# Attention's score rows spread over partitions through lines in DRAM, and a planner with other settings

## The chip, the cores and the metric

The kernel runs on one core of one Trainium2 chip. The metric is the device time of one execution in microseconds (us), the median of several runs. The core has five engines, each with a queue of its own that runs in order: PE (TensorE, matmuls; its weight loads are shown as PEld), DVE (VectorE), ACT (ScalarE), POOL (GpSimd) and SP (SyncE), which here only issues transfers (DMA). Engines meet through semaphores: an instruction that waits holds up everything behind it in its engine's queue.

## The reference

There are 128 graphs of 128 nodes with 256 features each, in float32, and an adjacency of 0 and 1 per graph. Four layers follow each other, each as `x = x + layer(relu(layernorm(x)))`.

```python
# layer 0: three GRU steps over the graph
m = einsum('bnd,de->bne', h, weight[i]); aggr = einsum('bst,bsd->btd', A, m)
h = gru_cell(aggr, h, w_ih, w_hh, b_ih, b_hh)
# layer 1: sum over neighbours by relation (adj holds the relation), times weight, plus bias
h = einsum('rbnm,bmd->rbnd', masks, x); y = einsum('rbnd,rdo->bno', h, weight) + bias
# layers 2 and 3: graph attention
Wh = einsum('bnd,od->bno', h, W)
e = leaky_relu((Wh @ a1)[:, :, None] + (Wh @ a2)[:, None, :], 0.2)
out = einsum('bij,bjo->bio', softmax(where(adj, e, -inf or -9e15)), Wh)
```

The score `e[i, j]` is the sum of one number of node i and one number of node j. With node i on the partition, the first is a number per partition, which an activation adds as its bias. The second is needed as a row of 128 numbers, the same on all partitions. The change is about how that row comes about.

## The kernel before

**Tiling.** Four graphs form a group (G = 4), so there are 32 groups (NG). A group's features are one tile of 128 x 4 x 256 in the pool `xs` (five buffers); its adjacency and the transposed adjacency come from `adjs` (seven). Intermediate 128 x 512 tiles come from `big` (27), statistics and small columns from `small` (ten), and PE writes into eight PSUM banks. `load` issues a group's four transfers on SP, and a store at the end of the group (L1096) writes the result.

**One group.** Layer 0 runs three GRU steps, whose matmuls are made of seven products in place of eight (`seventh`, L820); their bank is refilled several times, with a copy (`evict`, L330, on ACT or on DVE as the planner finds) or an add (L843, L898, L912) between. Layer 1 is `neighbours` (L624, L639). Layers 2 and 3 are `attention` with two masks. In `attention`, `norm` makes the normalised features (statistics on DVE from L532, one power on POOL at L558, the scaling on ACT at L574). Then `terms` (L993, DVE) takes two dot products per graph, which give the node's two score numbers as columns EI and EJ of a small tile. In `attend` the row is made on PE: a transpose of the column EJ, broadcast along the free dimension, against the identity (L1018). It lands in a bank, the same row on every partition. An activation adds EI (L1023, ACT); then follow the slope (L1027, DVE), the mask with a minimum (L1030), the exponential with its sum (L1036, ACT), the transpose of the weights (L1054, PE), two products (L1065, L1078) and the weighted add to the features (L1088, DVE).

**What sets the order.** Nothing is issued as it is written. `Plan.op` records each operation with an estimated duration; `Plan.order` then plays the program through and picks the next operation that could start first on its engine, by rank where several could. The rank is the group's number times PERIOD, less the length of the way to the group's end. At most AHEAD groups are open at once. SPARE keeps back buffers of some pools from groups that are not the oldest. LAG, HOP and OWN are the estimated times until the result of one engine is seen by another, or by itself. The order that comes out is written into the engines' queues and stays fixed. The last SPLIT groups are worked in two pieces of two graphs rather than whole.

**The branch.** A scan of the whole adjacency (32 transfers and reductions, L508 and L510) finds out whether it holds values above 1. The verdict (L513 to L519) goes to a branch: with 0 and 1 alone, layer 1 is `neighbours`; else the general `relations`. Work up to layer 0 is shared by both sides and may stand ahead of the branch.

Of the kernel before, what the change touches and what calls it, by code (L numbers as in the profile page):

```python
# [37 lines left out]
OWN = {"PE": 0, "ACT": 125, "DVE": 125, "POOL": 80, "SP": 0, "ACTQ": 0}  # L38
PERIOD = 28000
AHEAD = 4  # L40
SPLIT = 3
SPARE = (1, 0, 0, 3)
# [4 lines left out]
def seen(o, h):  # L47
    return LAG[o.eng] + HOP[h.eng] if h.engs != (o.eng,) else OWN[o.eng]


def act(n, ptrs=0):
    return 50 + 95 * ptrs + 0.833 * n


def dve(n):
    return 68 + n / 0.96
# [21 lines left out]
class Op:  # L78
    __slots__ = ("engs", "eng", "times", "ns", "fn", "deps", "heirs", "bufs", "group", "key", "port", "rank", "wait", "ready", "end")
# [12 lines left out]
class Plan:  # L92
# [6 lines left out]
    def op(self, eng, ns, fn, r=(), w=(), after=(), port=None):  # L99
# [4 lines left out]
        o.port = eng == "POOL" if port is None else port  # L104
        if self.shared:
            o.key = self.keys
            self.keys += 1
# [21 lines left out]
    def order(self, pools, cut=None, prefix=()):  # L129
# [37 lines left out]
        def place(o, eng, end):  # L167
# [85 lines left out]
def kernel(  # L253
# [40 lines left out]
    pools = [banks, xs, adjs, big, wide, half, small, mis]  # L294
# [3 lines left out]
    def build(general):  # L298
# [38 lines left out]
        def chunk(name):  # L337
            return Buf(big, name)
# [167 lines left out]
        for f in range(F):  # L506
# [7 lines left out]
            top.t[:, 0:1], most.t, AX.X, ALU.max), r=[most], w=[top])  # L514
        op("PE", 109, lambda: nc.tensor.transpose(pm.t[0:1, 0:P], top.t[:, 0:1], ident.t),
           r=[top, ident], w=[pm])
        op("DVE", 200, lambda: nc.vector.tensor_reduce(
            top.t[0:1, 1:2], pm.t[0:1, 0:P], AX.X, ALU.max), r=[pm], w=[top])
        verdict = op("DVE", 80, lambda: nc.vector.tensor_scalar(  # L519
            found, top.t[0:1, 1:2], 1.0, None, ALU.is_gt), r=[top])  # L520
# [5 lines left out]
        whole = (range(G),)  # L526

        def norm(xt, nm, pieces=whole):
# [39 lines left out]
            hs = []  # L568
            for g2 in range(G // 2):
                h = chunk(f"h{nm}{g2}")  # L570

                def scale(g2=g2, h=h):
                    for g in (2 * g2, 2 * g2 + 1):
                        nc.scalar.activation(  # L574
                            h.t[:, (g % 2) * D : (g % 2 + 1) * D], xt.t[:, g, :], AF.Relu,
                            bias=s.t[:, MR + g : MR + g + 1], scale=s.t[:, RS + g : RS + g + 1],
                        )

                op("ACT", 2 * act(D, 2) + 85, scale,
                   r=[(xt, {2 * g2, 2 * g2 + 1}), (s, {(n, g) for n in ("rs", "mr") for g in (2 * g2, 2 * g2 + 1)})], w=[h])  # L580
                hs.append(h)
# [16 lines left out]
        def bias(xt):  # L598
            for g2 in range(G // 2):
                op("POOL", 1370, lambda g2=g2: nc.gpsimd.tensor_tensor(  # L600
                    xt.t[:, 2 * g2 : 2 * g2 + 2, :], xt.t[:, 2 * g2 : 2 * g2 + 2, :],
                    b1s.t.unsqueeze(1).to_broadcast([P, 2, D]), ALU.add),
                   r=[b1s], w=[(xt, {2 * g2, 2 * g2 + 1})])
# [7 lines left out]
        def neighbours(gi, xt, ai, aiT, m0, m3, late, pieces):  # L611
# [4 lines left out]
            hs, _ = norm(xt, f"1_{gi}", pieces)  # L616
            bias(xt)
            for g2 in range(G // 2):
                pr = bank(f"pr{gi}{g2}")

                def gather(g2=g2, pr=pr):
                    for g in range(2):
                        for k in range(KC):
                            nc.tensor.matmul(  # L624
                                pr.t[:, (2 * k + g) * P : (2 * k + g + 1) * P],
                                hs[g2].t[:, g * D + k * P : g * D + (k + 1) * P],
                                mT.t[:, (2 * g2 + g) * P : (2 * g2 + g + 1) * P],
                                start=True, stop=True,
                            )

                op("PE", 892, gather, r=[hs[g2], mT], w=[pr])
                hr = chunk(f"hr{gi}{g2}")
                evict(T, lambda hr=hr: hr.t, lambda pr=pr: pr.t, r=[pr], w=[hr])
                py = bank(f"py{gi}{g2}")

                def mix(hr=hr, py=py):
                    for g in range(2):
                        for k in range(KC):
                            nc.tensor.matmul(  # L639
                                py.t[:, g * D : (g + 1) * D],  # L640
                                hr.t[:, (2 * k + g) * P : (2 * k + g + 1) * P],
                                w1s.t[:, k, :],
                                start=(k == 0), stop=(k == KC - 1),
                            )

                op("PE", 2 * KC * 2 * D * PE_COL, mix, r=[hr, w1s], w=[py])
                op("DVE", dve(T), lambda g2=g2, py=py: nc.vector.tensor_tensor(
                    xt.t[:, 2 * g2 : 2 * g2 + 2, :], xt.t[:, 2 * g2 : 2 * g2 + 2, :],
                    py.t.rearrange("p (g d) -> p g d", g=2), ALU.add),
                   r=[py], w=[(xt, {2 * g2, 2 * g2 + 1})])  # L650

        def relations(gi, xt, ai, aiT, m0, m3, late, pieces):
# [55 lines left out]
        def group(gi):  # L708
# [272 lines left out]
            pieces = (range(2), range(2, G)) if gi >= NG - SPLIT else whole  # L981
            (relations if general else neighbours)(gi, xt, ai, aiT, m0, m3, late, pieces)
            unrelated(m2, m0, FAR, late)

            def attention(i, mask):
                hs, s = norm(xt, f"{2 + i}_{gi}", pieces)

                EI, EJ = 48, 52
                for g in range(G):
# [9 lines left out]
                    op("DVE", 690, terms, r=[hs[g // 2], ub[i]], w=[junk, (s, {("ei", g)})], port=True)  # L999
# [3 lines left out]
            def attend(i, mask, hs, s, gs, EI, EJ):  # L1003
# [9 lines left out]
                pe, e = bank(f"pe{nm}"), chunk(f"e{nm}")  # L1013
# [7 lines left out]
                op("PE", 110 * len(gs), rows, r=[ident, (s, {("ei", g) for g in gs})], w=[pe])  # L1021
                for g in gs:
                    op("ACT", 250, lambda g=g: nc.scalar.activation(  # L1023
                        at(e, g), at(pe, g), AF.Identity, bias=s.t[:, EI + g : EI + g + 1]),
                       r=[pe, (s, {("ei", g)})], w=[(e, {g})])
# [33 lines left out]
                for g2 in range(gs.start // 2, gs.stop // 2):  # L1059
                    pc, c, po = bank(f"pc{nm}{g2}"), chunk(f"cT{nm}{g2}"), bank(f"po{nm}{g2}")  # L1060

                    def weigh(g2=g2, pc=pc):
                        for g in range(2):
                            for k in range(KC):
                                nc.tensor.matmul(  # L1065
                                    pc.t[:, (2 * k + g) * P : (2 * k + g + 1) * P],
                                    hs[g2].t[:, g * D + k * P : g * D + (k + 1) * P],
                                    at(eT, 2 * g2 + g),
                                    start=True, stop=True,
                                )  # L1070

                    op("PE", 892, weigh, r=[hs[g2], eT], w=[pc])
                    evict(T, lambda c=c: c.t, lambda pc=pc: pc.t, r=[pc], w=[c])

                    def transform(c=c, po=po):
                        for g in range(2):
                            for k in range(KC):
                                nc.tensor.matmul(  # L1078
                                    po.t[:, g * D : (g + 1) * D],
                                    c.t[:, (2 * k + g) * P : (2 * k + g + 1) * P],  # L1080
                                    wa[i].t[:, k, :],
                                    start=(k == 0), stop=(k == KC - 1),
                                )

                    op("PE", 2 * KC * 2 * D * PE_COL, transform, r=[c, wa[i]], w=[po])
                    for g in range(2):
                        gg = 2 * g2 + g
                        op("DVE", 395, lambda g=g, gg=gg, po=po: nc.vector.scalar_tensor_tensor(  # L1088
                            xt.t[:, gg, :], po.t[:, g * D : (g + 1) * D], s.t[:, RI + gg : RI + gg + 1],
                            xt.t[:, gg, :], ALU.mult, ALU.add),  # L1090
                           r=[po, (s, {("rinv", gg)})], w=[(xt, {gg})])
# [69 lines left out]
```

## Time and profile before

| what | us |
|---|---|
| median of three runs | 2647.51 (2646.8 to 2647.52) |
| the profiled execution | 2648.33 |
| its span, first to last instruction | 2646.5 |
| ACT busy | 1566.5 (59%) |
| POOL busy | 466.0 (18%) |
| 128 transfers of 256 KB for features and adjacency, issue to landing | 4.0 to 4.5 each |
| 29 stores of 512 KB | 3.3 each |

The profile comes from one execution. A group of instructions is shown by its line in the kernel, its engine, and its tiles. "Busy" counts the time in which an engine has an instruction under way; on PE instructions overlap, so the mean duration of one is longer than the time from one start to the next. The chain of waits is followed back from the last instruction, at each step to what released it, or to the instruction before it on its engine; what stands in it is what the end depended on. SP's queue in this kernel mostly stands still: it waited 2057.4 us in total before stores (L1096) for the last add of a group on DVE (L1088).

### The profile page before, as it was taken

How to read it: one execution, taken by the hardware profiler on the slowest of the kernel's cores; microseconds unless marked ns; L12 is line 12 of the kernel's file. 1: busy time of each engine (PE TensorE's matmuls, PEld its weight loads, DVE VectorE, ACT ScalarE, POOL GpSimd, SP SyncE). 2: the span in 40 equal slices, each digit the busy share in tenths (PEclk: the TensorE clock that was granted, in tenths of full speed). 3: DMA queues.
4: the chain of work that ended last, by engine and by line, in shares of the span. 5: the costliest groups of instructions: out<-in, count | busy, mean ns of one | idle time of the engine just before them, and what ended most of it. 6: DMA issues, size and time to landing. Idle time of an engine off the chain costs nothing.

```text
span 2646.5 us, 40354 instructions
## 1 busy us (share of the span) xinstructions
PE 2606.2 (98%) x14041; PEld 2321.0 (88%) x14041; DVE 2204.8 (83%) x6376; ACT 1566.5 (59%) x3792; POOL 466.0 (18%) x400
## 2 busy tenths in 40 slices
PE   8999999999999999999999999999999999999995
PEld 7888888888888888988898988888888889888884
DVE  8868898888888888888888888888888888888885
ACT  5446666656566565565565656565656655665553
POOL 1112122111121111121111111111111111211121
PEclk9999999999999999999999999999999999999997
DMA  6100000000000000000000000000000000000000
GB/s 208 42 1 1 29 21 25 25 25 25 10 16 25 25 25 25 1 25 25 25 25 25 1 25 25 25 25 21 5 25 25 25 25 2 24 25 25 9 9 18
DMA packets 77494, 65.22 MB, mean 25 GB/s; under 512 B 3936, under 2 KB 73184, under 8 KB 77280
## 3 DMA queue, kind: packets, MB, share of 16 engines
q1 hardware_dynamic: 76192, 61.50, 7.8%
q8 instruction: 112, 1.84, 0.3%
q10 hardware_dynamic: 1088, 1.05, 0.1%
q14 instruction: 102, 0.84, 0.1%
HBM read 45.75 MB, written 16.78 MB: 24 GB/s over the span
## 4 chain that ended last, share of the span: by engine, by line
PE 94%; DVE 4%; ACT 1%; issue 0%; DMA 0%; POOL 0%; ACTq 0%; DVEq 0%
PE bank L820 64%; PE bank L1078 8%; PE bank L1065 4%; PE bank L762 4%; PE bank L639 4%; PE bank L954 3%; PE bank L733 2%; PE bank L624 2%; PE bank L1054 1%; PE bank L1018 1%; DVE junk L993 0%; PE bank L445 0%; DVE small L532 0%; DVE big L922 0%; DVE big L942 0%
## 5 line engine op out<-in xcount | busy, mean ns | idle before, releaser
L330 ACT COPY big<-bank 128x512 f32<-128x512 f32 (+1 forms) x978 | 455.5, 481 | 496.7 <-PE bank L820 426.3
L820 PE MATMUL bank<-big,rz_h 128*128 128x256 f32 x1536 | 462.8, 383 | 0.3
L820 PE MATMUL bank<-big,rz_a 128*128 128x256 f32 x1536 | 456.8, 379 | 0.0
L929 POOL TENSOR_TENSOR big<-wide,big 128x512 f32<-128x512 f32 x192 | 245.6, 1298 | 1108.7 <-ACT big L927 951.6
L820 PE MATMUL bank<-wide,rz_h 128*128 128x256 f32 x1152 | 342.9, 379 | 0.3 <-DVE wide L330 0.3
L820 PE MATMUL bank<-wide,rz_a 128*128 128x256 f32 x1152 | 342.6, 379 | 0.0
L820 PEld LDWEIGHTS bank<-big,rz_a 128*128 128x128 f32 x1536 | 291.8, 190 | 39.8
L820 PEld LDWEIGHTS bank<-big,rz_h 128*128 128x128 f32 x1536 | 279.7, 190 | 47.3 <-ACT big L330 15.0
L558 POOL TENSOR_TENSOR small<-small,nhalf 128x4 f32<-128x4 f32 (+1 forms) x137 | 138.8, 1014 | 970.4 <-DVE small L556 951.6
L574 ACT ACTIVATE big<-xs,small 128x256 f32<-128x256 f32 x512 | 269.8, 592 | 48.4 <-DVE small L562 48.0
L837 ACT ACTIVATE big<-big,b_rz 128x256 f32<-128x256 f32 x576 | 258.2, 499 | 44.3 <-DVE big L843 42.1
L330 DVE COPY big<-bank 128x512 f32<-128x512 f32 (+1 forms) x276 | 159.9, 581 | 143.8 <-PE bank L820 89.3
L927 ACT ACTIVATE big<-big,bih_s 128x512 f32<-128x512 f32 x192 | 128.7, 715 | 205.4 <-DVE big L912 109.1
L820 PEld LDWEIGHTS bank<-wide,rz_a 128*128 128x128 f32 x1152 | 218.9, 190 | 29.7
L820 PEld LDWEIGHTS bank<-wide,rz_h 128*128 128x128 f32 x1152 | 216.3, 190 | 28.5 <-DVE wide L330 0.5
L1078 PE MATMUL bank<-wa,big 128*128 128x256 f32 x1024 | 235.5, 383 | 2.6 <-ACT big L330 2.6
L843 DVE TENSOR_TENSOR big<-bank,big 128x512 f32<-128x512 f32 x288 | 196.2, 686 | 47.3 <-PE bank L820 46.8
L820 PE MATMUL bank<-big,n_h 128*128 128x256 f32 x768 | 228.2, 380 | 0.8 <-DVE big L330 0.7
L1078 PEld LDWEIGHTS bank<-wa,big 128*128 128x128 f32 x1024 | 195.0, 191 | 30.6 <-ACT big L330 4.2
L820 PE MATMUL bank<-big,n_a 128*128 128x256 f32 x768 | 217.9, 379 | 0.0
L912 DVE TENSOR_TENSOR big<-bank,big 128x256 f32<-128x256 f32 x384 | 160.6, 419 | 61.6 <-PE bank L820 57.9
L993 DVE CUSTOM_DVE_ANT_0 junk<-big,ub 128x256 f32<-128x256 f32 x512 | 192.6, 421 | 1.6 <-ACT big L574 1.5
(91 smaller groups left out, 4723.0 us busy)
## 6 DMA issues: line engine op xcount, KB each, us to landing
xs<-in_x_dram SPq DMA_DIRECT2D x64, 256.0 KB, 4.0
out_dram<-xs SPq DMA_DIRECT2D x29, 512.0 KB, 3.3
adjs<-in_adj_dram SPq DMA_DIRECT2D x32, 256.0 KB, 4.3
adjs<-in_adjT_dram SPq DMA_DIRECT2D x32, 256.0 KB, 4.5
big<-in_adj_dram SPq DMA_DIRECT2D x32, 256.0 KB, 3.0
out_dram<-xs SPq DMA_DIRECT2D x6, 256.0 KB, 2.2
big<-in_wihT_dram ACTq DMA_DIRECT2D x3, 256.0 KB, 6.4
big<-in_whhT_dram SPq DMA_DIRECT2D x3, 256.0 KB, 5.8
```

The source lines that it names most:

```text
L330: (nc.scalar.copy if eng == "ACT" else nc.vector.tensor_copy)(dst(), src())
L558: op("POOL", 1130, lambda: nc.gpsimd.tensor_tensor(columns(RS), columns(RS), nhalf.t[:, gs.start : gs.stop], ALU.pow), r=[nhalf], w=[own(" ...
L574: nc.scalar.activation(h.t[:, (g % 2) * D : (g % 2 + 1) * D], xt.t[:, g, :], AF.Relu, bias=s.t[:, MR + g : MR + g + 1], scale=s.t[:, RS + ...
L639: nc.tensor.matmul(py.t[:, g * D : (g + 1) * D], hr.t[:, (2 * k + g) * P : (2 * k + g + 1) * P], w1s.t[:, k, :], start=(k == 0), stop=(k = ...
L820: nc.tensor.matmul(ps.t[:, m * W : (m + 1) * W], a.t[(slice(None), *row, j, slice(m * P, (m + 1) * P))], b[j](), start=(start and m == x = ...
L837: op("ACT", act(W, 1) + 40, lambda m=m, c=c: nc.scalar.activation(t[c].t[:, g2 * W : (g2 + 1) * W], src.t[:, m * W : (m + 1) * W], AF.Tanh ...
L843: op("DVE", dve(T), lambda: nc.vector.tensor_tensor(c.t, ps.t, c.t, ALU.add), r=[ps], w=[c])
L912: op("DVE", dve(W), lambda: nc.vector.tensor_tensor(dst(), ps.t[:, :W], dst(), ALU.add), r=[ps], w=[((ws if more else vs)[c], {g2})])
L927: op("ACT", act(T, 1) + 85, lambda nn=nn, c=c: nc.scalar.activation(nn.t, vs[c].t, AF.Tanh, bias=bi.t[:, 4 + c : 5 + c]), r=[vs[c], bi], w ...
L929: op("POOL", 1230, lambda qq=qq, nn=nn, c=c: nc.gpsimd.tensor_tensor(qq.t, hT.t[:, c, :], nn.t, ALU.subtract), r=[(hT, {(c, 0), (c, 1)}), ...
L993: nc.vector.tensor_tensor_reduce(out=junk.t[:, v * D : (v + 1) * D], in0=part, in1=ub[i].t[:, v, :], op0=ALU.mult, op1=ALU.add, scale=1.0, ...
L1078: nc.tensor.matmul(po.t[:, g * D : (g + 1) * D], c.t[:, (2 * k + g) * P : (2 * k + g + 1) * P], wa[i].t[:, k, :], start=(k == 0), stop=(k ...
```

## The change

The row no longer comes from PE for a group that is worked whole. SP writes the four columns EJ of the group (128 partitions x 4 floats, 16 bytes each) to a small tile in DRAM, `line`, so that the four numbers of a node stand next to each other. A second transfer reads this line of 2 KB once for each of the 128 partitions into a tile of `big`. The row of one graph is then every fourth float of it, and the activation that adds EI reads it with that step. There are four lines. Groups in pieces keep the transpose.

The planner's estimates get `late`, a time added to LAG for one operation: 5000 ns for the line, 2500 for the spread. An operation on SP that depends on another on SP now counts with 2500 in place of 0. PERIOD goes from 28000 to 26000, AHEAD from 4 to 5, SPLIT from 3 to 2, and SPARE no longer keeps a bank back. The four operations of the verdict get a rank that is 60000 earlier. Scaling, bias and the products are rewritten so that they could also run on single graphs; with SINGLE = 0 none does, and they run on pairs as before. The two products of layer 1 and of attention now share the function `product`.

```diff
-OWN = {"PE": 0, "ACT": 125, "DVE": 125, "POOL": 80, "SP": 0, "ACTQ": 0}
-PERIOD = 28000
-AHEAD = 4
-SPLIT = 3
-SPARE = (1, 0, 0, 3)
+OWN = {"PE": 0, "ACT": 125, "DVE": 125, "POOL": 80, "SP": 2500, "ACTQ": 2500}
+PERIOD = 26000
+AHEAD = 5
+SINGLE = 0
+SPLIT = 2
+LINE, SPREAD = 5000, 2500
+RUSH = 60000
+SPARE = (0, 0, 0, 3)
...
 def seen(o, h):
-    return LAG[o.eng] + HOP[h.eng] if h.engs != (o.eng,) else OWN[o.eng]
+    return o.late + (LAG[o.eng] + HOP[h.eng] if h.engs != (o.eng,) else OWN[o.eng])
...
-            o.rank = o.group * PERIOD - o.rank
+            o.rank = o.group * PERIOD - o.rank - o.rush
...
-                    last = max(u.end + LAG[u.eng] + 60 for u, _, _ in b.uses)
+                    last = max(u.end + u.late + LAG[u.eng] + 60 for u, _, _ in b.uses)
...
+    dram = ctx.enter_context(tc.tile_pool(name="dram", bufs=1, space=bass.MemoryType.DRAM))
+    lines = [dram.tile([P, G], F32, name=f"line_{j}") for j in range(4)]
+    pools = [banks, xs, adjs, big, wide, half, small, mis, lines]
...
         verdict = op("DVE", 80, lambda: nc.vector.tensor_scalar(
-            found, top.t[0:1, 1:2], 1.0, None, ALU.is_gt), r=[top])
+            found, top.t[0:1, 1:2], 1.0, None, ALU.is_gt), r=[top], rush=RUSH)
...
+        def product(gs, nm, hs, r, weight, w):
+
+            N = len(gs) * D
+            pc, c, po = bank(f"pc{nm}"), chunk(f"c{nm}"), bank(f"po{nm}")
+            op("PE", 446 * len(gs), lambda: sums(gs, pc, hs, weight),
+               r=[(hs[gs.start // 2], set(gs)), r], w=[pc])
+            evict(N, lambda: c.t[:, :N], lambda: pc.t[:, :N], r=[pc], w=[c])
+            op("PE", len(gs) * KC * 2 * D * PE_COL, lambda: mix(gs, po, c, w), r=[c, w], w=[po])
+            return po
...
-            pieces = (range(2), range(2, G)) if gi >= NG - SPLIT else whole
-            (relations if general else neighbours)(gi, xt, ai, aiT, m0, m3, late, pieces)
+            pieces = singly if gi >= NG - SINGLE else pairs if gi >= NG - SPLIT else whole
+            duos = singly if gi >= NG - SINGLE else pairs
+            (relations if general else neighbours)(gi, xt, ai, aiT, m0, m3, late, pieces, duos)
...
-                pe, e = bank(f"pe{nm}"), chunk(f"e{nm}")
+                e = chunk(f"e{nm}")
...
-                op("PE", 110 * len(gs), rows, r=[ident, (s, {("ei", g) for g in gs})], w=[pe])
+                terms = (s, {("ei", g) for g in gs})
+                if len(gs) == G:
+
+                    line, pe = Buf(lines, f"line{nm}"), chunk(f"pe{nm}")
+                    op("SP", 400, lambda: nc.sync.dma_start(out=line.t, in_=columns(EJ)),
+                       r=[terms], w=[line], late=LINE)
+                    op("SP", 1280, lambda: nc.sync.dma_start(
+                        out=pe.t, in_=line.t.rearrange("p g -> (p g)").partition_broadcast(P)),
+                       r=[line], w=[pe], late=SPREAD)
+
+                    def row(g):
+                        return pe.t[:, g : g + (P - 1) * G + 1 : G]
+                else:
+                    pe = bank(f"pe{nm}")
+                    op("PE", 110 * len(gs), rows, r=[ident, terms], w=[pe])
+
+                    def row(g):
+                        return at(pe, g)
                 for g in gs:
                     op("ACT", 250, lambda g=g: nc.scalar.activation(
-                        at(e, g), at(pe, g), AF.Identity, bias=s.t[:, EI + g : EI + g + 1]),
-                       r=[pe, (s, {("ei", g)})], w=[(e, {g})])
+                        at(e, g), row(g), AF.Identity, bias=s.t[:, EI + g : EI + g + 1]),
+                       r=[(pe, {g}), (s, {("ei", g)})], w=[(e, {g})])
```

More of the change, by code (lines that the diff above doesn't have):

```diff
@@ L78 @@
 class Op:
-    __slots__ = ("engs", "eng", "times", "ns", "fn", "deps", "heirs", "bufs", "group", "key", "port", "rank", "wait", "ready", "end")
+    __slots__ = ("engs", "eng", "times", "ns", "fn", "deps", "heirs", "bufs", "group", "key", "port", "rush", "late", "rank", "wait", "ready", "end")
     def __init__(self, engs, times, fn, group):
@@ L97, in __init__, with op @@
         self.keys = 0
-    def op(self, eng, ns, fn, r=(), w=(), after=(), port=None):
+    def op(self, eng, ns, fn, r=(), w=(), after=(), port=None, rush=0, late=0):
         o = Op(*((eng, ns) if isinstance(eng, tuple) else ((eng,), (ns,))), fn, self.group)
         o.port = eng == "POOL" if port is None else port
+        o.rush, o.late = rush, late
         if self.shared:
@@ L293 @@
     mis = pool(4, [P, G + 1, P], F32R, "mis")
-    pools = [banks, xs, adjs, big, wide, half, small, mis]
+    dram = ctx.enter_context(tc.tile_pool(name="dram", bufs=1, space=bass.MemoryType.DRAM))
+    lines = [dram.tile([P, G], F32, name=f"line_{j}") for j in range(4)]
+    pools = [banks, xs, adjs, big, wide, half, small, mis, lines]
     found = const.tile([1, 1], I32, name="found")
@@ L513, in build, with norm @@
         op("DVE", 120, lambda: nc.vector.tensor_reduce(
-            top.t[:, 0:1], most.t, AX.X, ALU.max), r=[most], w=[top])
+            top.t[:, 0:1], most.t, AX.X, ALU.max), r=[most], w=[top], rush=RUSH)
         op("PE", 109, lambda: nc.tensor.transpose(pm.t[0:1, 0:P], top.t[:, 0:1], ident.t),
-           r=[top, ident], w=[pm])
+           r=[top, ident], w=[pm], rush=RUSH)
         op("DVE", 200, lambda: nc.vector.tensor_reduce(
-            top.t[0:1, 1:2], pm.t[0:1, 0:P], AX.X, ALU.max), r=[pm], w=[top])
+            top.t[0:1, 1:2], pm.t[0:1, 0:P], AX.X, ALU.max), r=[pm], w=[top], rush=RUSH)
         verdict = op("DVE", 80, lambda: nc.vector.tensor_scalar(
-            found, top.t[0:1, 1:2], 1.0, None, ALU.is_gt), r=[top])
+            found, top.t[0:1, 1:2], 1.0, None, ALU.is_gt), r=[top], rush=RUSH)
         ST, MV, RS, NM, SU, RI, MR, DF = 0, 24, 32, 36, 40, 44, 56, 60
-        whole = (range(G),)
-        def norm(xt, nm, pieces=whole):
+        whole, pairs, singly = (
+            tuple(range(g, g + n) for g in range(0, G, n)) for n in (G, 2, 1))
+        def norm(xt, nm, pieces=whole, duos=pairs):
             s = Buf(small, f"s{nm}")
@@ L567, in norm, with scale @@
                 moments(gs)
[L568 to L573, printed above, removed]
+            hs = [chunk(f"h{nm}{g2}") for g2 in range(G // 2)]
+            for gs in duos:
+                def scale(gs=gs):
+                    for g in gs:
                         nc.scalar.activation(
-                            h.t[:, (g % 2) * D : (g % 2 + 1) * D], xt.t[:, g, :], AF.Relu,
+                            hs[g // 2].t[:, (g % 2) * D : (g % 2 + 1) * D], xt.t[:, g, :], AF.Relu,
                             bias=s.t[:, MR + g : MR + g + 1], scale=s.t[:, RS + g : RS + g + 1],
                         )
-                op("ACT", 2 * act(D, 2) + 85, scale,
-                   r=[(xt, {2 * g2, 2 * g2 + 1}), (s, {(n, g) for n in ("rs", "mr") for g in (2 * g2, 2 * g2 + 1)})], w=[h])
-                hs.append(h)
+                op("ACT", len(gs) * (act(D, 2) + 43), scale,
+                   r=[(xt, set(gs)), (s, {(n, g) for n in ("rs", "mr") for g in gs})],
+                   w=[(hs[gs.start // 2], set(gs))])
             return hs, s
@@ L595, in norm_halves, with bias, sums, mix @@
             return his, los
[L598 to L603, printed above, removed]
+        def bias(xt, duos=pairs):
+            for gs in duos:
+                op("POOL", 650 * len(gs), lambda gs=gs: nc.gpsimd.tensor_tensor(
+                    xt.t[:, gs.start : gs.stop, :], xt.t[:, gs.start : gs.stop, :],
+                    b1s.t.unsqueeze(1).to_broadcast([P, len(gs), D]), ALU.add),
+                   r=[b1s], w=[(xt, set(gs))])
+        def sums(gs, ps, hs, weight):
+            for j, g in enumerate(gs):
+                for k in range(KC):
+                    nc.tensor.matmul(
+                        ps.t[:, (len(gs) * k + j) * P : (len(gs) * k + j + 1) * P],
+                        hs[g // 2].t[:, (g % 2) * D + k * P : (g % 2) * D + (k + 1) * P],
+                        weight(g), start=True, stop=True,
+                    )
+        def mix(gs, ps, c, w):
+            for j in range(len(gs)):
+                for k in range(KC):
+                    nc.tensor.matmul(
+                        ps.t[:, j * D : (j + 1) * D],
+                        c.t[:, (len(gs) * k + j) * P : (len(gs) * k + j + 1) * P],
+                        w.t[:, k, :], start=(k == 0), stop=(k == KC - 1),
+                    )
+        def product(gs, nm, hs, r, weight, w):
[6 more added lines that the diff above has]
+            return po
         def unrelated(m, m0, far, late):
@@ L609, in unrelated, with neighbours @@
                 AF.Copy, bias=far, scale=-far), r=[m0], w=[m], after=late)
-        def neighbours(gi, xt, ai, aiT, m0, m3, late, pieces):
+        def neighbours(gi, xt, ai, aiT, m0, m3, late, pieces, duos):
             mT = chunk(f"mT{gi}")
@@ L615, in neighbours @@
             unrelated(m3, m0, -NEG_INF, late)
[L616 to L650, printed above, removed]
@@ L652, in relations @@
-        def relations(gi, xt, ai, aiT, m0, m3, late, pieces):
+            hs, _ = norm(xt, f"1_{gi}", pieces, duos)
+            bias(xt, duos)
+            for gs in duos:
+                py = product(gs, f"{gi}_1{gs.start}", hs, mT, lambda g: mT.t[:, g * P : (g + 1) * P], w1s)
+                op("DVE", dve(len(gs) * D), lambda gs=gs, py=py: nc.vector.tensor_tensor(
+                    xt.t[:, gs.start : gs.stop, :], xt.t[:, gs.start : gs.stop, :],
+                    py.t[:, : len(gs) * D].rearrange("p (g d) -> p g d", d=D), ALU.add),
+                   r=[py], w=[(xt, set(gs))])
@@ L655, in relations @@
+        def relations(gi, xt, ai, aiT, m0, m3, late, pieces, duos):
             ai = Buf(adjs, f"again{gi}")
@@ L980, in group @@
             late = [o for o, _, _ in hT.uses[:1]]
-            pieces = (range(2), range(2, G)) if gi >= NG - SPLIT else whole
-            (relations if general else neighbours)(gi, xt, ai, aiT, m0, m3, late, pieces)
+            pieces = singly if gi >= NG - SINGLE else pairs if gi >= NG - SPLIT else whole
+            duos = singly if gi >= NG - SINGLE else pairs
+            (relations if general else neighbours)(gi, xt, ai, aiT, m0, m3, late, pieces, duos)
             unrelated(m2, m0, FAR, late)
             def attention(i, mask):
-                hs, s = norm(xt, f"{2 + i}_{gi}", pieces)
+                hs, s = norm(xt, f"{2 + i}_{gi}", pieces, duos)
                 EI, EJ = 48, 52
@@ L997, in terms @@
                             )
-                    op("DVE", 690, terms, r=[hs[g // 2], ub[i]], w=[junk, (s, {("ei", g)})], port=True)
+                    op("DVE", 690, terms, r=[(hs[g // 2], {g}), ub[i]], w=[junk, (s, {("ei", g)})], port=True)
                 for gs in pieces:
@@ L1057, in attend @@
                 evict(N, lambda: eT.t[:, :N], lambda: pp.t[:, :N], r=[pp], w=[eT])
[L1059 to L1091, printed above, removed]
@@ new lines, in attend @@
+                for duo in duos:
+                    if duo.start not in gs:
+                        continue
+                    po = product(duo, f"{nm}{duo.start}", hs, eT, lambda g: at(eT, g), wa[i])
+                    for j, g in enumerate(duo):
+                        op("DVE", 395, lambda j=j, g=g, po=po: nc.vector.scalar_tensor_tensor(
+                            xt.t[:, g, :], po.t[:, j * D : (j + 1) * D], s.t[:, RI + g : RI + g + 1],
+                            xt.t[:, g, :], ALU.mult, ALU.add),
+                           r=[po, (s, {("rinv", g)})], w=[(xt, {g})])
```

## The prediction

> **What bounds the kernel now.** I read the page's first view (busy time), then a table of stretches of the span, then the chain of waits, then groups and transfers.
>
> ```profile
> PE 2606.2 (98%) x14041; PEld 2321.0 (88%) x14041; DVE 2204.8 (83%) x6376; ACT 1566.5 (59%) x3792; POOL 466.0 (18%) x400
> ```
>
> ```profile
> 1420.00:1500.00 80.00, 80.00 (x437) 71.62 (x435) 67.47 (x195) 48.62 (x119) 14.06 (x13) 1.00 0.07 21
> 1500.00:1580.00 80.00, 80.00 (x437) 71.63 (x436) 67.47 (x195) 48.63 (x119) 14.05 (x13) 1.00 0.07 21
> ...
> 2560.00:2580.00 20.00, 19.16 (x99) 16.22 (x97) 14.31 (x49) 9.13 (x26) 2.31 (x2) 1.00 0.00 1
> 2580.00:2600.00 20.00, 12.54 (x61) 10.45 (x62) 13.03 (x62) 11.95 (x30) 5.98 (x7) 0.66 0.00 0
> 2600.00:2620.00 20.00, 12.60 (x54) 9.57 (x53) 12.36 (x61) 6.91 (x20) 1.53 (x3) 0.83 0.08 27
> 2620.00:2646.50 26.50, 13.22 (x48) 9.35 (x47) 8.96 (x43) 6.90 (x20) 1.27 (x2) 0.74 0.07 24
> ```
>
> The stretches give length, then busy PE, PEld, DVE, ACT and POOL, the granted clock and the DMA. In the middle PE has no idle time; DVE has 12.5 us of 80 free and ACT 31.4. PE idles only at the two ends: 8.2 us in the first 20, and 0.84 + 7.46 + 7.40 + 13.28 = 29.0 us after 2560. A group of four graphs comes every 80.17 us (in the chain a run of 36 L820 matmuls recurs at 1330.39, 1410.56, 1490.73). So what leaves PE's queue in the middle leaves the time, if nothing new makes PE wait.
>
> The chain of waits has the price of what is removed (start, us, what):
>
> ```profile
> 1418.33 1.78 PE bank L624 x16
> 1420.11 0.44 PE bank L1018 x4
> 1420.55 1.73 PE bank L820 x8
> ...
> 1433.18 6.91 PE bank L820 x32
> ...
> 1452.20 0.44 PE bank L1018 x4
> ```
>
> Four score transposes take 0.44 us of the path, twice a group: 0.11 us each. An L820 matmul takes 0.216 (6.91 / 32). The groups view shows a mean of 278 ns for L1018; that is an overlapping latency, not what it costs.
>
> ```profile
> L1018 PE MATMUL bank<-ident,small 128*128 128x128 f32 x256 | 40.7, 278 | 6.7 <-DVE small L993 6.7
> L1023 ACT ACTIVATE big<-bank,small 128x128 f32<-128x128 f32 x256 | 78.0, 375 | 8.7 <-PE bank L1018 8.6
> L1036 ACT ACTIVATE big<-big,small 128x128 f32<-128x128 f32 x256 | 100.2, 396 | 40.9 <-DVE small L1030 37.6
> ```
>
> ```profile
> xs<-in_x_dram SPq DMA_DIRECT2D x64, 256.0 KB, 4.0
> adjs<-in_adjT_dram SPq DMA_DIRECT2D x32, 256.0 KB, 4.5
> small<-in_a_dram SPq DMA_DIRECT2D x2, 2.0 KB, 4.9
> ```
>
> The last number of each transfer is its median time from issue to landing, in us.
>
> **What the Trainium skill says.** "Perfetto Trace Analysis", section Identifying the Most-Contended Engine, calls matmul busy time a bad metric, since matmuls overlap: this trace agrees (278 ns shown, 110 ns from start to start), so I price by starts. "DMA: Bandwidth & Descriptors", Rules for kernel authors, says that a transfer that reads what an earlier one wrote must wait on the first one's semaphore: the two new transfers are strictly one after the other; nothing in the trace of before has such a pair. Its Specifications put transfers under 512 B below line rate, with a read-modify-write: the line is 128 pieces of 16 B. The nearest row, 128 pieces of 16 B read rather than written, landed in 4.9 us. "SBUF — State Buffer", section Door 1, says that SBUF has 16-byte lines and an access to a new line pays a penalty: the new rows are read with a step of 4 floats, 16 B. No row of the trace has such a read.
>
> **The change, part by part.**
>
> 1. Removed: L1018's transposes of the whole groups. With SPLIT 2, groups 0 to 29 are whole: 30 x 2 x 4 = 240 of 256 leave PE. 240 x 0.11 = 26.4 us, 0.88 a group. All of them but those near the end stand where PE has no gap. Group 29, cut into two pieces before, becomes whole; its PE work is otherwise equal, and it saves some short DVE, ACT and POOL work beside a full PE.
>
> 2. Added: 60 lines and 60 spreads on SP's queue. An issue there took 0.34 to 0.5 us in the rows of that queue; 120 of them are 60 us of 2600 on an engine that in before spends 2057 us waiting at L1096. Bytes: 60 x 256 KB on top of 65 MB, with the DMA engines 7% busy in the middle. Hidden. The two in a row take, by the nearest rows, 4.9 + 4.0 to 4.9 = about 10 us; bounds are 5 us (two at the 2.2 us of a 256 KB store, plus issue) and 15 us with the queue's waits. The wait is on ACT, at the first activation that reads the row; behind it in ACT's order stand the evictions PE waits for, so lateness there reaches PE at once. The cover is in the program's order. Between a group's last dot product and the first activation on its row, the changed order has PE work of 19.7 us for the first attention and 26.0 us for the second in the middle groups, and 14.6 to 16.0 us at the thinnest (groups 0, 28, 29), counted at 0.11 and 0.216 us. Against 10 us all of it is hidden, with 4 us to spare at worst; at 15 us it just holds. Cost taken: 0.
>
> 3. SP's order. In the middle it is line (second attention), store of the finished group, line of the next group's first attention, four loads, then both spreads. The spread thus stands behind a store that waits on DVE for the last residual add of its group (L1088) and loads that wait for that store to land (3.3 us). This is inside the 19.7 and 26.0 us. The loads themselves are for a group three later; nobody is near them.
>
> 4. ACT reads rows from SBUF with a step instead of a bank: 375 ns before; 396 for the same size from contiguous SBUF (L1036). Bounds: 20 ns less, to 107 ns more if every element costs a further cycle (an estimate from L330, where 256 further columns take 585 - 372 = 213 ns, so 128 take 107). At 8 a group that is at most 0.86 us of ACT's 31.4 free. Cost 0 by itself.
>
> 5. Planner: five groups in flight, period 26000, spares. It moves work on every engine but adds no PE instruction. The returns PE -> copy or add -> PE are what can open gaps. In before's order three of these a group have only 0.86 to 0.87 us of PE work between (bank Y, V), and PE has no gap in the middle. The chain's tail shows what they need: 0.04 + 0.59 + 0.04 us for a 512-column copy on ACT, so 0.86 leaves 0.19. The changed order has six such returns at 0.86 to 0.89. I charge the three more 0.01 us each: 3 x 0.01 x 30 = 1 us. If each loses all 0.19 and as much again (a late ACT): up to 0.4 us a group, 12 us.
>
> 6. The verdict on the adjacency (L510 to L519) gets RUSH. In before it fell at 225.1 us although the last scan ended at 103.8. In the changed order the branch stands after PE work of 147 us (215 before), some 157 us into the span, still 50 us behind that scan, so PE should not wait there. Cost 0; up to 5 us if the branch's own wait shows.
>
> 7. The end. PE's order after group 31's last transposes is the same list but for small swaps, and the last two groups keep their PE rows and halves. Its 29 us of idle time stays; plus or minus 4 us for how groups 30 and 31 interleave.
>
> Sum against the profiled execution: span 2646.5 - 26.4 + 1 = 2621.1; with the 1.8 us around it (2648.33 - 2646.5) 2622.9. The median of the runs, 2647.51, is 0.8 below that execution's time: 2622.
>
> **Rivals.**
>
> A, forecast: transfers hidden, PE's saving kept. 2622, own range 2612 to 2632 (the end's 4 us, the branch's 5, and a few returns either way). For it: the full middle stretches and the cover of 15 us or more.
>
> B, part given back: the tighter returns of step 5 with later ACT rows of step 4. 12 us: 2634. For: six instead of three. Against: before lost nothing at the same 0.86.
>
> C, given back whole: gaps of 0.88 us a group; 2647. It needs twice what B has at its worst.
>
> D, slower: the round trip through DRAM outlasts the cover. Place: the first activation on a spread row, with the evictions queued behind it on ACT. Price: each us late costs up to 1 us of PE at each of 60 places. Break-even is 26.4 / 60 = 0.44 us late on average, a round trip of some 20 to 23 us where rows suggest 10. One us late: 2622 + 60 = 2682. Against: even the contended transfers at the start landed in 4.9 to 6.4 us. For: 16-byte writes, one line read 128 times, and a store with a DVE wait ahead of the spread were never measured here.
>
> **How the numbers follow.** A 0.72, B 0.11, C 0.05, D 0.12. Less than 0.2% (5.3 us) cannot be told from no change. Faster is A and B, 0.83; same 0.05; slower 0.12. The range runs from A's low end, 2612, to 2638, which takes in B; C's and D's 0.17 are left out.
>
> **What would show it.** Right: the L1018 line falls to 16; a period near 79.3 us between equal L820 runs; PE full in the middle stretches; line and spread landing in 10 us together; no wait of ACT for the spread tile above 1 us in total; the end's idle near 29 us. Wrong: ACT waiting on a DMA at the row activations followed by PE waiting for L330 copies (D); many PE waits of 0.1 to 0.3 us for L330 or L912 (B, C); an idle stretch near 157 us (step 6).

## The result and the profile after

The changed kernel takes 2654.05 us (median of 8 runs, 2651.03 to 2655.78) against 2647.48 before (2646.8 to 2647.64). The ratio is 1.0024, with a 95% interval of 1.0013 to 1.0035: a little slower, where 2622 was forecast. The 240 transposes did leave PE, but the kernel lost 32 us elsewhere that the forecast didn't count.

The page of after, busy time; then the stretches in the middle and near the end, with the columns as before (length, busy PE, PEld, DVE, ACT, POOL, clock, DMA):

```profile
PE 2600.2 (98%) x13801; PEld 2289.9 (86%) x13801; DVE 2194.3 (83%) x6298; ACT 1596.7 (60%) x3845; POOL 535.0 (20%) x397
```

```profile
480.00:560.00 80.00, 79.25 (x424) 70.00 (x423) 66.41 (x190) 49.81 (x120) 17.70 (x12) 1.00 0.09 27
...
2160.00:2240.00 80.00, 79.25 (x426) 69.96 (x425) 66.15 (x191) 49.80 (x120) 17.68 (x12) 1.00 0.09 27
```

PE has 240 matmuls fewer, but it is no longer full in the middle: in these stretches 0.75 us of 80 are idle, and ACT and POOL are busier than before. The clearest measure is the period, from one group's store to the next. SP's order in time (start, us) gives it over 19 groups, before:

```profile
644.65 0.38 SPq L1096 DMA_DIRECT2D out_dram<-xs  x1
...
2168.24 0.38 SPq L1096 DMA_DIRECT2D out_dram<-xs  x1
```

and after:

```profile
644.17 0.39 SPq L1102 DMA_DIRECT2D out_dram<-xs  x1
...
2178.20 0.39 SPq L1102 DMA_DIRECT2D out_dram<-xs  x1
```

Before, a period is (2168.24 - 644.65) / 19 = 80.19 us; after, 80.74. With 0.88 us less on PE it should be 79.31. So 1.43 us a group are lost, 27 us over these 19 periods. The span is 32.5 us longer than forecast (2653.6 against 2621.1); the other 5 lie before and after this stretch.

The transfers of after, and who waited for what over the whole span:

```profile
big<-line SPq DMA_DIRECT2D x60, 256.0 KB, 5.2
adjs<-in_adj_dram SPq DMA_DIRECT2D x32, 256.0 KB, 5.2
line<-small SPq DMA_DIRECT2D x60, 2.0 KB, 1.4
```

```profile
DVE mis L730 <- DMA adjs<-in_adj_dram: 65.7, 27, 3.3
...
DVE small L573 <- POOL small L569: 36.8, 43, 1.1
...
PE bank L832 <- DVE big L924: 6.4, 14, 0.8
...
PE bank L832 <- ACT big L338: 5.7, 10, 0.7
```

Line and spread land in 1.4 + 5.2 us and no engine that computes waits for the spread: the round trip is hidden. Three other things are new. DVE waits 27 times, 2.4 us on average, for the adjacency of a later group (L730). The power of the normalisation (L569) is slower. And the rows themselves are slower on ACT (L1053 by line and tile, ns as min/median/max):

```profile
L1053 ACT ACTIVATE big<-big,small x240: 507/533/591, 194.0 to 2534.2; 128x128 f32<-128x128 f32 x120
...
L1053 ACT ACTIVATE big<-bank,small x16: 347/367/391, 2570.1 to 2640.2; 128x128 f32<-128x128 f32 x16
```

The same activation takes 533 ns when it reads every fourth float of the spread tile and 367 from a bank. Here is one place where PE stops; first PE, then ACT in the same microseconds (start, length, what, idle time before):

```profile
1472.92 1.29 PE L745 MATMUL bank<-mis,half 128*128 128x256 f32 x8
1474.77 0.70 PE L832 MATMUL bank<-big,n_h 128*128 128x256 f32 x2 [0.56 <-ACT big L338]
```

```profile
1472.85 0.93 ACT L1053 ACTIVATE big<-big,small 128x128 f32<-128x128 f32 x2
1473.68 0.35 ACT L338 COPY wide<-bank 128x256 f32<-128x256 f32 x1
1473.94 0.52 ACT L1053 ACTIVATE big<-big,small 128x128 f32<-128x128 f32 x1
1474.36 0.35 ACT L338 COPY big<-bank 128x256 f32<-128x256 f32 x1
```

PE waits for the copy of 1474.36, ahead of which ACT works through three rows without a gap, each 0.42 us from start to start. The planner had put 250 ns on a row. Before, four rows of L1023 took 1.13 us together, about 0.25 each from start to start:

```profile
1420.61 1.13 ACT L1023 ACTIVATE big<-bank,small 128x128 f32<-128x128 f32 x4
```

### The profile page after: what moved, and what is told of

Its sections match the earlier page's. It is cut to its first block, busy times and chain, and to the rows that moved or that the text cites. A ratio compares the mean times of both kernels' runs of the same rounds, so it can differ in the third digit from the quotient of the medians.

```text
span 2653.6 us, 40230 instructions
## 1 busy us (share of the span) xinstructions
PE 2600.2 (98%) x13801; PEld 2289.9 (86%) x13801; DVE 2194.3 (83%) x6298; ACT 1596.7 (60%) x3845; POOL 535.0 (20%) x397
## 4 chain that ended last, share of the span: by engine, by line
PE 77%; DVE 11%; ACT 7%; DMA 3%; issue 1%; ACTq 0%; DVEq 0%
PE bank L832 52%; PE bank L628 11%; PE bank L618 6%; PE bank L774 3%; DVE junk L1006 3%; DMA adjs<-in_adj_dram 3%; PE bank L966 2%; PE bank L745 2%; ACT big L583 2%; ACT big L1053 1%; DVE big L805 1%; DVE big L811 1%; DVE xs L1094 1%; ACT big L1066 1%; ACT big L849 1%; ACT wide L338 1%
## 5 line engine op out<-in xcount | busy, mean ns | idle before, releaser
L338 ACT COPY big<-bank 128x256 f32<-128x256 f32 (+1 forms) x1002 | 462.0, 479 | 534.7 <-PE bank L832 371.4
L569 POOL TENSOR_TENSOR small<-small,nhalf 128x4 f32<-128x4 f32 (+1 forms) x134 | 194.0, 1448 | 1430.8 <-DVE small L567 1382.8
L941 POOL TENSOR_TENSOR big<-wide,big 128x512 f32<-128x512 f32 x192 | 255.9, 1346 | 625.5 <-ACT big L939 328.4
L832 PE MATMUL bank<-big,n_a 128*128 128x256 f32 x768 | 227.9, 382 | 8.3 <-DVE big L924 6.4
L338 DVE COPY big<-bank 128x512 f32<-128x512 f32 (+1 forms) x250 | 148.1, 594 | 82.5 <-PE bank L966 37.0
L618 PEld LDWEIGHTS bank<-big,big 128*128 128x128 f32 x1536 | 186.7, 193 | 17.9 <-DVE big L338 9.5
L954 DVE SCALAR_TENSOR_TENSOR big<-big,big 128x512 f32<-128x512 f32 x192 | 153.2, 834 | 56.5 <-POOL big L941 34.9
```

The costliest lines, as they stand in the source:

```text
L338: (nc.scalar.copy if eng == "ACT" else nc.vector.tensor_copy)(dst(), src())
L569: op("POOL", 1130, lambda: nc.gpsimd.tensor_tensor(columns(RS), columns(RS), nhalf.t[:, gs.start : gs.stop], ALU.pow), r=[nhalf], w=[own(" ...
L618: nc.tensor.matmul(ps.t[:, (len(gs) * k + j) * P : (len(gs) * k + j + 1) * P], hs[g // 2].t[:, (g % 2) * D + k * P : (g % 2) * D + (k + 1) ...
L832: nc.tensor.matmul(ps.t[:, m * W : (m + 1) * W], a.t[(slice(None), *row, j, slice(m * P, (m + 1) * P))], b[j](), start=(start and m == x = ...
L941: op("POOL", 1230, lambda qq=qq, nn=nn, c=c: nc.gpsimd.tensor_tensor(qq.t, hT.t[:, c, :], nn.t, ALU.subtract), r=[(hT, {(c, 0), (c, 1)}), ...
L954: op("DVE", dve(T) + 125, lambda c=c, qq=q[c]: nc.vector.scalar_tensor_tensor(qq.t, t[2 + c].t, 1.0, qq.t, ALU.add, ALU.mult), r=[t[2 + c] ...
```

## The experiments

Three causes are in question: the adjacency load (L), the rows' step (R), and the planner's settings (P), to which the slow power (W) was added on the way. Periods below are made as above, from the stores at about 640 and 2170 us of the one execution that was profiled. Most plans have even periods; in after, e1, e11, e12 and e14 they vary, and there a mean is good to some 0.2 us (the executions of e11 or of e12 differ by 6 us, over some 25 periods).

**e1_near** reads the row without the step:

```diff
-                        return pe.t[:, g : g + (P - 1) * G + 1 : G]
+                        return pe.t[:, g * P : (g + 1) * P]
```

> Only the step of the row's read goes: the activation reads 128 neighbouring floats of the spread tile in place of every fourth, so a graph's scores are made with the wrong nodes' numbers; order, transfers and all other work are those of after. Theory L (the adjacency load, which stands behind the next group's line on SP, reaches DVE some 2 us late each period): the rows get shorter on ACT but the lateness stays; 2648 to 2655. Theory R (the stepped read, 533 ns against 375, puts 8 x 0.16 = 1.26 us a group on ACT ahead of evictions that PE waits for): 27 periods lose 1.26 us less, 2654 - 34 = 2620, the floor without stalls. If both stand in one chain with some slack, 2620 to 2630. Theory P (the planner's settings make an order with too tight returns): 2650 or more.

2635.72 us, ratio to before 0.9956 (0.9939 to 0.9972), period 80.08. So in the changed kernel the step costs 18 us of the 32. The row by line and tile, from the same tile without the step:

```profile
L1053 ACT ACTIVATE big<-big,small x240: 384/412/456, 193.9 to 2515.8; 128x128 f32<-128x128 f32 x120
```

412 ns against 533: the step is 121 ns of each row, and the place (SBUF instead of a bank, 367) 45. It isn't all: 0.8 us a period remain above 79.3.

**e2_hoist** moves the loads of adjacency and transposed adjacency on SP, and nothing else. After the plan is made, each goes ahead of whatever stands between it and the last spread, unless that still uses its buffer:

```diff
+    issue = issue[:cut] + hoist(issue, cut)[cut:]
     with tc.manual_schedule():
```

> Only the place of the adjacency loads on SP changes: they go right behind the two spreads before them, ahead of both lines and the store; every other engine keeps its order. Theory L: DVE's wait at the mask for the adjacency (65.7 us in all) goes to near 0 and the period falls from 80.9 to about 79.3; 2620 to 2625. Theory R: the wait goes, PE still waits behind the rows; 2648 to 2655. Both in one chain: 2620 to 2630. Theory P: 2650 or more.

2658.13 us, period 80.85. DVE's wait for the adjacency is gone; by its tile:

```profile
L730 DVE TENSOR_SCALAR mis<-adjs x32: 405/416/428, 8.0 to 2408.8; 128x512 fp32r<-128x512 int32 x32
...
  DMA adjs<-in_adj_dram: 1.0, 1
```

65.7 us of waiting went to 1.0 and the time didn't fall. DVE's largest new wait cost nothing here, so theory L falls for the kernel as it is. One reason shows only with theory W below: with the loads on time, more of the powers are slow. Between 600 and 2200 us, 38 of 79 take over 1.5 us, against 28 of 79 in after.

**e4_oldplan** has rows through DRAM with the five settings of before.

> Rows through DRAM as in after, with the planner's settings of before: four groups at work, period 28000, one bank kept back, three groups in pieces, no rush. Theory P: the removed transposes now count; 29 whole groups save 25.5 us, about 2622. Theories L and R: the order is another, so the lateness may fall elsewhere, but the rows still cost 0.16 us each more; 2630 to 2660.

2722.18 us, ratio 1.0282 (1.0265 to 1.0299): outside all expectations. The period is 80.6, but PE starves when the attention of the first groups begins:

```profile
260.00:300.00 40.00, 31.81 (x167) 28.29 (x167) 32.34 (x103) 24.75 (x49) 16.37 (x14) 0.87 0.05 7
300.00:340.00 40.00, 26.00 (x122) 21.41 (x120) 28.86 (x100) 18.83 (x44) 8.37 (x7) 0.83 0.05 14
340.00:380.00 40.00, 25.20 (x118) 22.11 (x119) 23.65 (x95) 18.41 (x50) 2.02 (x2) 0.74 0.20 53
```

37 us of PE are idle in these 120, more than the transposes cost altogether. So the rows through DRAM are worse still with the settings of before. Which of the five does it wasn't tried. In the middle, the stops of PE that its profile shows lie at other short returns, with no row ahead in the chain that was read.

**e5_perows** has after's settings and the rows on PE (`if False:` in place of `if len(gs) == G:`).

> Rows by transposes on PE as in before, with the planner's settings of after. Theory P: slower than before by what after lost, 2647 + 33 = 2680, or at least above 2655. Theories L and R: no line stands ahead of the loads and no row is read with a step; 2640 to 2650, as before.

2657.45 us, ratio 1.0036 (1.0024 to 1.0049), period 80.37 against 80.19. The settings alone cost 0.18 us a period, and the rest of the 10 us is at the ends. Yet the profile has PE busy throughout:

```profile
600.00:1000.00 400.00, 399.98 (x2174) 357.22 (x2173) 342.17 (x998) 233.10 (x558) 73.18 (x60) 1.00 0.07 21
```

A record of a 256-column matmul is 0.38 us long while the next starts 0.216 later, so a gap of up to 0.16 us shows as busy.

**e3_near_hoist** joins e1 and e2.

> e1_near and e2_hoist together: the row's read takes neighbouring floats (a graph's scores are made with the wrong nodes' numbers), and the adjacency loads stand ahead of the lines. Theory R+L (the late load costs nothing while the rows hold ACT up, and shows once they do not): period from e1_near's 80.0 to 79.3 or 79.5, 2617 to 2625. Theory R+P (what e1_near still loses, 80.0 - 79.3 = 0.7 us a period, lies in the order's tight returns alone): 2633 to 2638, as e1_near.

2635.56 us, every period but one 80.1 (mean 80.05). The load isn't the rest either. The chain of waits of this run shows another delay:

```profile
1454.77 0.08 DVE small L567
1454.86 0.07 issue
1454.92 2.34 POOL small L569
1457.26 0.02 issue
1457.29 0.17 DVE small L573
1457.46 0.02 issue
1457.48 2.08 ACT big L583 x4
```

The power takes 2.34 us; then come scaling, casts, rows and the copy that PE waits for. After has it too. POOL and DVE in the same microseconds:

```profile
1464.44 2.33 POOL L569 TENSOR_TENSOR small<-small,nhalf 128x4 f32<-128x4 f32 x1 [24.02 <-DVE small L567]
```

```profile
1464.29 1.28 DVE L934 SCALAR_TENSOR_TENSOR big<-big,big 128x512 f32<-128x512 f32 x2
1465.49 0.41 DVE L928 TENSOR_TENSOR big<-big,big 128x256 f32<-128x256 f32 x1
1466.80 0.16 DVE L573 SCALAR_TENSOR_TENSOR small<-small 128x4 f32<-128x4 f32 x1 [0.90 <-POOL small L569]
```

The power is under way while DVE runs three instructions with two inputs in SBUF, and ends 0.87 us after the last of them. Before, all 80 powers between 600 and 2200 us took 1.01 to 1.13 us, as this one:

```profile
1461.62 1.01 POOL L558 TENSOR_TENSOR small<-small,nhalf 128x4 f32<-128x4 f32 x1 [8.99 <-DVE small L556]
```

The Trainium skill, "SBUF — State Buffer", section "SBUF: two separate sides", says that DVE and GpSimd share a pair of ports under an exclusive lock, which a DVE operation with two SBUF inputs takes against a GpSimd operation that reads SBUF. The trace agrees in time and shows the size: 2.3 to 2.7 us in place of 1.0, for two of a group's four powers in e3 (39 of 80) and for 28 of 79 in after. It isn't so each time: at 1302.48 us of after a power beside the same three instructions takes 1.39 us. What decides between the two isn't known. The planner gives the power 1130 ns and, by `port=False`, no share in the lock.

**e8_told_rows** leaves the stepped rows and tells the planner what they cost:

```diff
-                    op("ACT", 250, lambda g=g: nc.scalar.activation(
+                    op("ACT", 410, lambda g=g: nc.scalar.activation(
                         at(e, g), row(g), AF.Identity, bias=s.t[:, EI + g : EI + g + 1]),
```

> The stepped read stays; only the planner is told 410 ns for a row in place of 250, so the order is planned anew. Theory R as stated so far (the order, made with 250, has evictions right behind the rows): an order that reckons with the rows regains most of it, 2625 to 2640. Rival (ACT's time itself is the loss, wherever it stands): 2650 to 2656.

2631.16 us, ratio 0.9939 (0.9922 to 0.9955), period 79.36: the forecast's, to 0.1 us. The rows are as slow as ever (median 560 ns) and PE is full:

```profile
600.00:1000.00 400.00, 400.00 (x2161) 357.16 (x2160) 338.54 (x977) 251.77 (x599) 79.10 (x63) 1.00 0.10 27
```

So it was not ACT's total time but the order, which had been made for rows of 250 ns. This version beats both kernels. But the new order takes away more than the delay behind the rows: no power between 600 and 2200 us is longer than 1.39 us, though the planner was told nothing of them, and DVE waits for the adjacency only 3.6 us in all. Nobody aimed at these two, and how the gain divides among rows, powers and loads isn't shown.

**e6_layout** lays the line out graph by graph, so that the row is contiguous; the line is then written in 512 pieces of 4 B. **e10_layout_loads** also tells the planner of 2500 ns more for the loads.

> The line is laid out graph by graph (each partition writes four pieces of 4 B, 512 in all), so that the row is contiguous in the spread tile and read without a step; nothing else changes, the planner's estimates and order neither. Theory R: as e1_near, 2632 to 2640, if the line lands within the cover; the line's landing goes from 1.4 us to perhaps 2 to 4. Rival (the small pieces are too slow): the spread comes late, ACT waits at the row, above 2650.

> e6_layout, and the planner is told 2500 ns more for the landing of the group's loads (measured 5.2 to 5.6 us against 3.8 reckoned); planned anew. Theory R+L: 2616 to 2628, below both kernels. Rival (another order, other tight returns): 2630 to 2645.

2893.93 and 2821.72 us. (What e10 computes is wrong, by a fault that was not found, so only its waits are read here.) The line's landing, in e6:

```profile
line<-small SPq DMA_DIRECT2D x60, 2.0 KB, 10.9
```

The same 2 KB took 1.4 us in pieces of 16 B. Of e6's waits the largest on DVE is this:

```profile
DVE mis L730 <- DMA adjs<-in_adj_dram: 257.1, 28, 12.1
```

The loads that stand behind the lines make DVE wait up to 12 us, and now it counts. That is the forecast's rival D with another victim: in e6 not the rows, but the next group's adjacency. In e10 D comes true at its own place as well, the row's activation on ACT:

```profile
ACT big L1053 <- DMA big<-line: 72.2, 19, 5.3
```

**e11_near_pow** and **e12_pow** put a multiply on DVE where the power was, with and without the near rows:

```diff
-                op("POOL", 1130, lambda: nc.gpsimd.tensor_tensor(
-                    columns(RS), columns(RS), nhalf.t[:, gs.start : gs.stop], ALU.pow),
+                op("POOL", 1130, lambda: nc.vector.tensor_tensor(
+                    columns(RS), columns(RS), nhalf.t[:, gs.start : gs.stop], ALU.mult),
```

> e1_near (rows read without the step, so a graph's scores are made with the wrong nodes' numbers), and the power of the normalisation (POOL) is left out: a multiply of the same size on DVE, 0.15 us, stands in its place, so the features are scaled wrongly. The order of all else is that of after. Theory W (two of a group's four powers meet two-input DVE work on SBUF, take 2.3 to 2.7 us in place of 1.0, and the rest of e1_near's 80.0 - 79.3 = 0.7 us a period comes from that): period 79.3 to 79.4, about 2617 to 2622. Rival P (the 0.7 lies in tight returns): 2632 to 2637.

> The power alone is left out in that way, the stepped rows stay. If both delays stand in one chain of about 1.3 + 1.4 us of which some 1.1 is covered: period 79.7 to 80.1, 2628 to 2638. If the rows alone decide: 80.7, 2650 to 2655.

2634.9 and 2648.24 us; both miss what was expected. e11 looked like the end of theory W (period 80.0 as in e1), but its periods are uneven: many are 79.5 long, some 80.2 and more, one 83.5. The few waits of PE (4.9 us between 600 and 2200, for L924) fall on DVE, which waits 48.8 us in that stretch for the adjacency. In e12 the quiet periods are 79.9. So the load was put ahead again.

**e15_near_pow_hoist** and **e16_pow_hoist**:

> Rows without the step (a graph's scores are made with the wrong nodes' numbers), the power left out (a DVE multiply of the same size in its place), and the adjacency loads ahead of the lines. Theory C (rows and power hold up one chain through ACT; the load adds only where they are gone): every period 79.4 to 79.5, 2618 to 2624. Rival P (0.7 us a period in tight returns): 79.8 or more, 2630 or more.

> The power left out and the loads ahead, the stepped rows stay. Theory C: every period near 79.9 (the quiet ones of e12_pow), so 2630 to 2638; with e3_near_hoist (80.1, power without rows) and e2_hoist (80.9, both) the two add up to more than each alone. If the rows alone are covered now: 79.5, 2622.

2625.53 us (ratio 0.9916, 0.9899 to 0.9932), 1.5 us above the expected range, and 2637.36 us, inside it. The periods are even now, 79.53 and 79.94. Eight kernels that share one order but for these edits give the account of a period:

| rows with step | power on POOL | load behind the lines: period | load ahead: period |
|---|---|---|---|
| yes | yes | 80.74 (after) | 80.85 (e2) |
| no | yes | 80.08 (e1) | 80.05 (e3) |
| yes | no | 80.38 (e12) | 79.94 (e16) |
| no | no | 80.00 (e11) | 79.53 (e15) |

With the load ahead: power alone 0.52 us over e15, rows alone 0.41, both 1.32, more than their sum. This fits one chain through ACT that both lengthen and that covers a part of one delay, but not of the second; the cover itself wasn't measured. The power's 0.52 is that of the whole step on POOL as it stands in this order, not of the collisions alone. The late load costs 0.4 to 0.5 us, but only without the power; the medians say the same, 9 and 11 us less with the load ahead in the last two rows, nothing and 4 us more in the others. What e15 still has above 79.31, 0.22 us, is probably a short return: in its chain the first product's 16 matmuls (L618) take 2.04 us once, where elsewhere they take 1.78.

**e14_told_loads**, a control to e8: another plan, with 2500 ns more for the loads and 250 for a row.

> Control to e8_told_rows: the planner is told 2500 ns more for the landing of a group's loads and keeps 250 ns for a row, planned anew. Theory R: rows are still reckoned too short, so the period stays above 79.8; 2635 to 2660. Rival (any new plan mends it by chance, or the late load was the cause): 79.3 to 79.5 a period, 2620 to 2632.

2656.61 us, period 80.42. So a new plan as such doesn't mend it. But it is a weak control: what it computes is wrong, by a fault that was not found, and PE's stops lie at other short returns in it; in the chains that were read, at most one row stands ahead of them. A run between the two, with 330 ns for a row (e18), gave no time: the planner found no order for it.

**e13_told_split3** and **e17_told_rows_pow** are e8 with three groups in pieces, and with the power's port told (`port=False` taken away).

> The planner is told 410 ns for a row, as in e8_told_rows, and three groups are worked in pieces in place of two, as before. Middle as in e8, 79.4 a period. The last full group at the end of e8 has idle PE of 6 us at 2340 to 2440; if that is the line's and spread's way to go at the end, 2623 to 2628; if any switch to pieces costs it, 2630 to 2634.

> The planner is told 410 ns for a row and, besides, that the power shares DVE's port, so that it plans no collision. e8_told_rows has 79.4 a period without it, so the middle can give nothing more: 2626 to 2634, by the end alone. If it matters: below 2626.

2637.4 and 2636.65 us, both above the expected ranges, with periods of 79.34 both. e17's middle is another order than e8's (e13's is the same), so two orders made with 410 ns reach the forecast's period. Nothing is left to gain in the middle. Both end later than e8: two groups in pieces are better than three by 6 us. Why e17 ends later wasn't looked at, and 2631.16 stays the best version found.

## Why the prediction failed, by its own steps

1. **Removal: right.** L1018's successor is down to 16 matmuls, and 0.88 us a group is what it was worth: e8 has 79.36 where 80.19 - 0.88 = 79.31.

2. **Round trip: right.** The two landings are 1.4 + 5.2 us. With the queue's other transfers between them the way is longer, about 12 us where SP's order was read (line issued at 1449.38, spreads from 1456.19 us; an estimate, 6.8 + 5.2), a little above the 10 taken and inside the cover of 14.6 us and more. Rival D's place, ACT at the row, never waited for the spread.

3. **SP's order: wrong in its last sentence.** "Nobody is near them": L730 is. The loads stand behind the next group's line, and land in 5.2 us rather than the 4.3 of before, with the two spreads in the queue. It cost nothing in the changed kernel (e2) and some 0.45 us a group without the power (e16, e15).

4. **The rows: the step that failed.** The bound was 107 ns more for each; it is 533 - 375 = 158 in duration, of which 121 are the step's own (e1), and 0.17 us from start to start. It was estimated from the price of further columns. The Trainium skill's page that the prediction cites here ("SBUF — State Buffer", section Door 1) names a penalty for each access to a new 16-byte line, without a figure; the trace agrees, with these 121 ns for 128 columns. But a right size would not have saved the step. It set 0.86 us against 31.4 us of ACT that are free in an average period. Those are not free where the rows stand: there ACT goes from scaling through casts and rows to copies for PE without a gap, in an order planned for 250 ns. The measured price is 18 us in the changed kernel (e1), where the step was put at 0; it is 0.41 us a group where the power doesn't delay the same chain (e16 over e15).

5. **The planner: mis-sized.** Three more short returns were charged 0.01 us each. What is left in e15 and may be theirs is 0.22 us a group, some 6 us in all and not 1. The worst case was also added up for too little: three returns that each lose 0.19 us and as much again are 1.1 us a group, some 34 us, where the prediction has 0.4 and 12. That the new order brings up to two powers a group beside two-input work on DVE was not seen at all: the power's step is 0.52 us a group alone, and with the rows 0.52 + 0.41 + 0.39.

6. **The branch: right.** PE is full from 140 to 180 us.

7. **The end: right.** PE idles 30.6 us after 2320 where before had 30.8 after 2240.

Rival B named late rows and short returns, and its 12 us were a third of what they and the power took. Rival C's 0.88 us of gaps a group was held to need twice B's worst, by the sum that was too small; 1.43 came.

## What to carry to other kernels

In a kernel whose order is planned ahead, an operation that gets slower can be paid for twice: in its own time, and in the order that was made with the old figure. Measure it and give the planner the new one before judging the change; here the order made with that one number was 23 us faster, though part of this may be luck with the powers. Idle time of an engine counts only at the place where the slower work stands, so look at what runs there and what is queued behind it. And a large new wait in a profile may be worth nothing until the delays it lies beside are gone.

## What was not expected of the hardware

- A ScalarE read of 128 x 128 floats from SBUF with a step of 16 B takes 533 ns; without the step 412 (e1), from PSUM 367. A step of four floats isn't free.
- 2 KB from SBUF to DRAM landed in 1.4 us as 128 pieces of 16 B, and in 10.9 us as 512 pieces of 4 B.
- PE busy for the whole of a stretch does not mean that nothing waits: e5, e15 and e8 show 399.98, 400.00 and 400.00 of 400 us, with periods of 80.37, 79.53 and 79.36 (e5 holds 8 transposes more, worth 0.88).
